# Where two groups of indirect gathers and the edge-row selection stand in the last two segments of a segmented attention kernel

## The chip, the cores and the metric

The kernel runs on one NeuronCore of a Trainium2 chip. The time is the device time of one execution in microseconds (us). Five engines work side by side, each through its own instruction stream in order: PE (matrix products), ACT (activations and copies), DVE (elementwise work and reductions), POOL (here it mostly issues indirect DMAs) and SP (plain DMAs). They meet only through semaphores.

## The reference, cut to what matters

```python
q, k, v = feat @ Wq, feat @ Wk, feat @ Wv            # feat: 16384 x 256
starts = searchsorted(bids, arange(8))               # bids are not sorted
pos = arange(N) - starts[bids]
qp, kp, vp = (zeros((8, 3072, .)).at[bids, pos].set(x) for x in (q, k, v))
attn = softmax(where(mask, qp @ kp^T, -1e9))         # within each of 8 segments
r = (attn @ vp)[bids, pos]
t = r @ Wt
tn = (t - t.mean(0)) / sqrt(t.var(0) + 1e-5) * gamma + beta
return feat + relu(tn)
```

Since `bids` is not sorted, most tokens have a `pos` outside 0..3071. Such tokens read the first or last row of a segment (the "edge" rows). Two tokens can also fall on the same place; the one that loses reads the winner's row. So each attention row is read some number of times, and the mean and the variance over all tokens are sums over attention rows weighted by how often each is read.

## The kernel before, in words

The fast path (`fast_path`, from L902) gathers the rows that own a place, segment by segment, into `xs`: up to six tiles of 128 rows for each of NB = 8 segments (FT = 6). In this data segment 7, and segment 6 too, have at most 512 rows, so the matmuls of their tiles 4 and 5 are skipped by predicates. Segment e is worked through in steps u = 0..5 (`step`, L1675): `attend` (L1270) multiplies the exponentiated scores `pa`/`pb` with the values `vs` into PSUM and DVE takes the reciprocal of the row sums into `rdens`; `scale` (L1285) writes the normalised rows `tk` (even u on ACT, odd u on DVE; in segment 7 all on ACT) and, after u = 3 and u = 5, SP stores them to the DRAM table `t_rows`. Between the steps of segment e stands the preparation of segment e+1: transposes `xT`, projections `q` and `k`, `values` and `scores`. Everything is written out by hand in one order; `Program.op` (L588) turns overlaps of tiles into semaphore waits, and each engine runs its own part of the order strictly in sequence.

For the moments, `past` (L1685) takes finished tiles from a list `lag`: ACT squares a tile (`square`, L1299), DVE adds the tile and its square into `acc`, weighted by the read counts `reads_r` (`moments`, L1329).

POOL's order in the last two segments matters here. It issues, one after the other:

- the read counts: `gather_reads(7, u)` (L1197), six gathers of 128 counts from the table `reads_of`, one in each `attend(6, u)`, each tied to that step's reciprocal (`paced`, L1279);
- `ridl`, three gathers of row numbers for the losing tokens;
- `late[1]`, that is `h` (L1627): six elementwise products on POOL that build the selection matrices `sel` from `edge`; `edge` comes from `late[0]`, that is `f` (L1598), a small matmul and a few small DVE instructions. Both stand after `step(6, 3)` (L1813);
- `tl`, the rows read a second time: three gathers from `t_rows`, rows of segments 0 to 5 only (L1829), after `step(6, 5)`. Line 1861 gathers them again from the whole table after the last segment, for the output;
- `ecat`, the edge rows: one gather from `t_rows` (L1743) in segment 7 after `step(7, 0)`, tied to `eidx`, the last instruction of `f`.

Segment 7 runs in the order u = 0, 1, 4, 5, 2, 3. After `step(7, 0)` the three `tl` tiles are put at the head of `lag` (L1752), so ACT squares `tl` next and DVE adds it. At u = 4 `weigh` (L1635) adds the read counts of tiles 2 and 3 to the edge weights, in `rw`. At u = 2 PE forms the edge rows of segment 7 (`sel` times `tk`, L1775), DVE adds them to `ecat` (L1778) and ACT squares `ecat`. After the last segment PE adds everything into `sums` (L1867, L1868), DVE transposes it (`st_t`, L1875), and a chain of small instructions gives scale and shift. Then the output phase starts: 16 groups of 1024 tokens are loaded, added, and stored by SP (`load_group`, `store`), while POOL scatters the 39 tiles of owned rows and losers (`put`), the tiles of a segment only when the group stores below it have landed.

SP also loads token groups during the last two segments: groups 0 to 2 in segment 6, groups 3 to 5 after `step(7, 0)` (L1744), group 6 after `step(7, 5)` (L1755), groups 7 to 9 after the loop. In the same queue stand the stores of `tk` to `t_rows`.

PSUM: `nb()` (L1050) hands out two banks in turn. `f`, `values`, `project`, `g` and `g2` take theirs from it.

Of the kernel before, what the change touches and what calls it, by code (L numbers as in the profile page):

```python
# [21 lines left out]
NB = 8  # L22
# [7 lines left out]
FW = FT * P  # L30
LT = 3
# [870 lines left out]
def fast_path(nc, feat, bids, wq, wk, wv, wt, gamma, beta, out, bad):  # L902
# [10 lines left out]
    pg = Fast(nc)  # L913
# [57 lines left out]
    xl, tl = new("xl", [P, LT, D]), new("tl", [P, LT, D])  # L971
# [16 lines left out]
    eidx, ridl, idxo = new("eidx", [P, 1], I32), new("ridl", [P, LT], I32), new("idxo", [P, LT], I32)  # L988
# [208 lines left out]
    def gather_reads(e, t, after):  # L1197
        m = e * FT + t
        pg.gather(reads_r[:, m : m + 1], reads_of, idx[:, m : m + 1], N, after=[after])

    def over4(e, t):
        return None if t < 4 else (e, t - 3)

# [40 lines left out]
    def values(e, c):  # L1244
        b = nb()
        for i in range(2):
            t = 2 * c + i
            for h in range(DH):
                pg.mm(
                    b[:, i * D : (i + 1) * D], xT[:, h, t * P : (t + 1) * P], wvt[:, h, :],  # L1250
                    start=(h == 0), stop=(h == DH - 1), pred=over4(e, t),
                )
        pg.copy("ACT", vs[e % 2][:, 2 * c : 2 * c + 2, 0:D], b[:].rearrange("p (t d) -> p t d", t=2))

    def scores(e, c, tiles):
        qe, ke = q[e % 2], k[e % 2]
        dst, n = (pa, QA) if c == 0 else (pb, QB)
        for t in tiles:
            g = slice(32 * (t % 4), 32 * (t % 4) + 32)
            pg.mm(  # L1260
                ps_s[t % 4][:, 0:n], ke[g, t // 4, :], qe[g, c * QA : c * QA + n],
                pred=over4(e, max(t, 4 * c)),
            )
        for t in tiles:
            m = e * FT + t
            pg.act(dst[:, t, :], ps_s[t % 4][:, 0:n], AF.Exp, bias=mask[:, m : m + 1])
# [3 lines left out]
    def attend(e, u):  # L1270
        po = po_of[u] = nb() if e == NB - 1 and u in (2, 3) else ps_o[u % 2]
        src, w = (pa, u) if u < 4 else (pb, u - 4)
        for t in (0, 1, 2, 4, 5, 3):
            pg.mm(
                po[:, 0 : D + 1], src[:, t, w * P : (w + 1) * P], vs[e % 2][:, t, :],
                start=(t == 0), stop=(t == 3), pred=over4(e, max(t, u)),
            )
        m = e * FT + u
        paced = pg.recip(rdens[:, m : m + 1], po[:, D : D + 1])  # L1279
        if EARLY_B <= e + 1 < NB:  # L1280
            gather_reads(e + 1, u, paced)
        if u % 2 and e < NB - 1:
            pg.ts(tk[:, m, :], po[:, 0:D], rdens[:, m : m + 1], ALU.mult)

# [390 lines left out]
    def step(e, u, more=None):  # L1675
        attend(e, u)
        if more is not None:
            more()
        scale(e, u)
        if (e, u) != (NB - 1, 1):  # L1680
            lag.append((e, u))
# [36 lines left out]
    for e in range(NB):  # L1718
        last = e == NB - 1
        n = e + 1  # L1720
        if e == 1:
            one, two, three_ = edges()
            sides = [*side_count(0, below[:]), *side_count(1, above[:])]
            fills = fill_rows()
            work.extend([fills[0], *one, fills[1], two, *sides, fills[2], *three_, lambda: own_of(NB - 1)])
        if not last:
            size_of(n)
        pg.region_of((e,) if last else (e, n))
        if e == 0:
            xt_rest(0)  # L1730
            values(0, 1)
            project(0, 1)
            values(0, 2)
            scores(0, 0, range(4, 6))
            own_of(2)
            zero_fill(2)
        if last:
            for u in (0, 1, 4, 5, 2, 3):
                step(e, u)
                if u == 0:  # L1740
                    scores(e, 1, range(4))
                    late[2]()
                    pg.gather(ecat[:, 0, :], t_rows[0 : (NB - 1) * FW, :], eidx[:], (NB - 1) * FW)  # L1743
                    for g in range(FIRST, EARLY):  # L1744
                        load_group(g)
                if u == 1:
                    scores(e, 1, range(4, 6))
                    late[4]()
                if u == 4:
                    late[3]()  # L1750
                if u == 0:
                    lag[:0] = [(NB, t) for t in range(LT)]  # L1752
                if u == 5:
                    first = square(e, 1)
                    for g in range(EARLY, MID):  # L1755
                        load_group(g)
                if u == 1:
                    pg.act(row_sum[:], ones[:], AF.Identity, scale=reads_r[:, e * FT + 1 : e * FT + 2])
                if u == 3:
                    any_ = hot[0 : 2 * NB, 0:2, :, :].rearrange("p k u x -> p (k u x)")  # L1760
                    pg.mm(sums[:], none[0 : 2 * NB, :], any_, start=True, stop=False)
                    by_row(row_sum, first[0], first[2])
                if u == 3:
                    while lag or squared:
                        if lag and len(squared) < 2:
                            squared.append(square(*lag.pop(0)))
                        else:
                            moments()
                else:
                    past(e)  # L1770
                if u == 2:
                    b_e = ps_s[0]
                    for u_ in (0, 4, 5, 1):
                        pg.mm(
                            b_e[:, 0:D], sel[:, u_, :], tk[:, e * FT + u_, :], start=(u_ == 0), stop=(u_ == 1),  # L1775
                            pred=over4(e, u_),
                        )
                    pg.tt(ecat[:, 0, :], ecat[:, 0, :], b_e[:, 0:D], ALU.add)  # L1778
                    pg.act(ecat[:, 1, :], ecat[:, 0, :], AF.Square)
        else:  # L1780
            busy = e + 2 < NB
            step(e, 0, lambda: (xt_main(n, 0), xt_main(n, 1)))
            if e + 3 < NB:
                prefix(e + 2, e + 3)
                sizes(e + 2)
            if busy:
                list_ahead(e + 2)
            scores(e, 1, range(4))
            past(e)
            slot()  # L1790
            if e == NB - 2:
                load_group(0)
            step(e, 1)
            xt_rest(n)
            project(n, 0)
            if busy:
                list_part(e + 2, 0)
            scores(e, 1, range(4, 6))
            past(e)
            slot(1 if busy else 2)  # L1800
            step(e, 2, lambda: project(n, 1))
            if busy:
                list_part(e + 2, 1)
            past(e)
            slot(1 if busy else 2)
            if e == NB - 2:
                slot(99)
                load_group(1)
                load_group(2)
            if e + 3 < NB:  # L1810
                zero_fill(e + 3)
            step(e, 3)
            if e == NB - 2:  # L1813
                late[0]()
                late[1]()
            scores(n, 0, range(4))
            step(e, 4, lambda: values(n, 0))
            past(e)
            if e + 4 < NB:
                own_of(e + 3)  # L1820
            if not busy:
                slot(2)
            if e == 3:
                losers()[0]()
            slot()
            step(e, 5)
            if e == NB - 2:
                for t in range(LT):
                    pg.gather(tl[:, t, :], t_rows[0 : EARLY_B * FW, :], ridl[:, t : t + 1], EARLY_B * FW)  # L1829
            values(n, 1)  # L1830
            past(e)
            if e == 3:
                losers()[1]()
            if e == NB - 4:
                prefix(NB - 1, NB)
                sizes(NB - 1)
                pg.copy("DVE", armf[:], arm[:])
                pg.red(cnt_f[0:1, 0:1], armf[:])
                pg.ts(upto[:, NB + 1 : NB + 2], cnt_f[0:1, 0:1], 16.0, ALU.mult, 16.0 * (4 * NB + LT), ALU.add)
                todo, late = rows()  # L1840
                work.extend(todo)
            scores(n, 0, range(4, 6))
            values(n, 2)
            past(e)
            slot()
        if last:
            assert not lag and not squared
        pg.end_region()
        if e == NB - 2:
            slot(99)  # L1850
            pg.set("POOL", none[:], 0.0)
# [227 lines left out]
```

## Time and profile before

| | |
|---|---|
| runs | 327.79 us median of 5 (327.03 to 328.62) |
| profiled execution | 326.57 us, of which the span from first to last instruction is 322.0 us |
| busy share of the span | PE 77%, DVE 74%, PEld 51%, ACT 47%, POOL 42% |
| mean granted TensorE clock | 0.893 |
| POOL groups | reads_r gather 12 times, 1056 ns each; tl gather 6 times, 1031 ns; ecat gather once, 1015 ns; sel 6 times, 858 ns |
| segments 0 to 6 | up to about 211 us |
| segment 7 and the sums | about 211 to 234.5 us |
| scale and shift | 234.5 to 241.9 us |
| output phase | 241.9 us to the end |

All times in what follows are microseconds from the start of the span. In the timeline and in the chain of waits, the first number is when an instruction (or a run of equal ones) starts and the second how long it lasts; a bracket gives how long its engine stood idle before it and what ended that. In the table by windows, the columns are the busy time of PE, PEld, DVE, ACT and POOL in a window (with the number of instructions), the granted TensorE clock (1.00 is full speed), the mean busy share of the 16 DMA engines, and GB/s.

### The profile page before, as it was taken

What the parts mean: (1) busy time and instruction counts of PE and PEld (TensorE: products, weight loads), DVE (VectorE), ACT (ScalarE), POOL (GpSimd) and SP (SyncE); (2) the same over time, 40 slices, a digit from 0 to 9 for tenths busy, and PEclk for the clock granted to TensorE, in tenths of its full rate; (3) what the DMA queues carried; (4) which work ended last, traced back from release to release, by engine and by line L of the source; (5) the groups of instructions that cost most, each with busy time, mean ns of one, the idle gap of its engine ahead of it and who ended that gap; (6) DMA issues with size and microseconds to landing.
All of it is one profiled execution on the core that took longest, in us unless ns stands there. A gap on an engine that the chain in (4) does not pass through costs nothing.

```text
span 322.0 us, 4632 instructions
## 1 busy us (share of the span) xinstructions
PE 247.8 (77%) x1279; PEld 163.2 (51%) x1279; DVE 239.3 (74%) x773; ACT 150.8 (47%) x294; POOL 135.9 (42%) x143
## 2 busy tenths in 40 slices
PE   5599799998998999899989999790956955642500
PEld 2465566666676678667866776470612322210100
DVE  3845679988577686569577898952879999999920
ACT  3037868775674674376448639671701221110000
POOL 7343316070170052404402563684030247878773
PEclk9999899999999999999999999797785797775755
DMA  3111104133063015301210134497598899999894
GB/s 103 29 29 34 34 2 136 43 105 93 0 124 132 0 51 135 95 0 52 71 35 1 51 108 139 166 344 283 189 413 327 302 381 423 417 415 380 331 379 170
DMA packets 21533, 52.49 MB, mean 163 GB/s; under 512 B 5488, under 2 KB 14786, under 8 KB 17530
## 3 DMA queue, kind: packets, MB, share of 16 engines
q1 hardware_dynamic: 15674, 41.37, 34.3%
q0 software_dynamic: 5280, 10.18, 10.8%
q10 hardware_dynamic: 544, 0.52, 0.5%
q8 instruction: 15, 0.25, 0.3%
q14 instruction: 20, 0.16, 0.1%
HBM read 26.27 MB, written 28.74 MB: 171 GB/s over the span
## 4 chain that ended last, share of the span: by engine, by line
PE 49%; DVE 21%; ACT 9%; issue 8%; POOL 7%; DMA 2%; another core or an unknown queue 1%; POOLq 1%; DVEq 0%; SPq 0%
PE ps L803 47%; POOL out L894 4%; DVE f L822 4%; DVE tk L822 4%; ACT pa L813 3%; PE ps L808 2%; DMA tl<-t_rows,ridl 2%; ACT xT L813 2%; ACT vs L818 2%; DVE junk L829 1%; DVE k L819 1%; DVE tk L1933 1%; DVE tk L1935 1%; ACT xs L818 1%
## 5 line engine op out<-in xcount | busy, mean ns | idle before, releaser
L878 POOL DMA_INDIRECT xs<-in_r_feat,idx x48 | 50.9, 1061 | 99.3 <-DVE idx L842 51.1
L803 PE MATMUL ps<-vs,pa 128*128 128x257 f32 x312 | 78.3, 396 | 4.1 <-ACT vs L818 3.8
L803 PEld LDWEIGHTS ps<-vs,pa 128*128 128x128 f32 x312 | 58.4, 195 | 18.0 <-ACT vs L818 6.2
L894 POOL DMA_INDIRECT out<-tk,idx x32 | 36.6, 1145 | 27.9 <-DVE f L822 15.9
L803 PE MATMUL ps<-wvt,xT 128*128 128x256 f32 x156 | 38.2, 393 | 0.7 <-ACT vs L818 0.7
L818 ACT COPY f<-ps 128x1024 f32<-128x1024 f32 (+1 forms) x12 | 10.0, 835 | 58.1 <-PE ps L803 58.1
L803 PE MATMUL ps<-y,hot 32*128 32x256 bf16 x256 | 14.5, 357 | 28.0 <-DVE f L822 19.9
L803 PEld LDWEIGHTS ps<-wvt,xT 128*128 128x128 f32 x156 | 29.6, 195 | 11.6 <-ACT sq L813 2.3
L813 ACT ACTIVATE pa<-ps,mask 128x512 f32<-128x512 f32 x48 | 29.5, 687 | 11.1 <-PE ps L803 10.3
L803 PEld LDWEIGHTS ps<-y,hot 32*128 32x128 bf16 x256 | 6.6, 113 | 44.8 <-DVE f L822 28.1
L803 PE MATMUL ps<-f,ident 128*128 128x512 f32 x38 | 27.3, 842 | 2.2 <-DVE f L822 1.2
L822 DVE TENSOR_TENSOR f<-f,ps 128x1024 f32<-128x1024 f32 (+3 forms) x17 | 26.0, 1560 | 3.8 <-remote 2.9
L819 DVE COPY k<-ps 32x128 f32<-32x128 f32 x48 | 14.1, 294 | 14.5 <-PE ps L803 13.8
L813 ACT ACTIVATE xT<-ps,negx 128x512 f32<-128x512 f32 (+1 forms) x32 | 16.9, 582 | 16.9 <-PE ps L808 10.0
L818 ACT COPY vs<-ps 128x512 f32<-128x512 f32 x24 | 14.1, 589 | 22.2 <-PE ps L803 17.4
L813 ACT ACTIVATE q<-ps,cqk 96x512 f32<-96x512 f32 (+3 forms) x32 | 18.3, 573 | 9.8 <-PE ps L803 9.5
L878 POOL DMA_INDIRECT reads_r<-reads_of,idx x12 | 12.7, 1056 | 24.3 <-DVE ge L831 11.7
L855 DVE RECIPROCAL rdens<-ps 128x1 f32<-128x1 f32 x48 | 7.7, 161 | 20.3 <-PE ps L803 20.3
L842 DVE SCALAR_TENSOR_TENSOR acc<-tk,reads_r,acc 128x256 f32<-128x256 f32 x45 | 21.6, 480 | 1.5 <-issue 1.3
L842 DVE SCALAR_TENSOR_TENSOR acc<-sq,reads_r,acc 128x256 f32<-128x256 f32 x45 | 21.5, 478 | 0.0
L813 ACT ACTIVATE pb<-ps,mask 128x256 f32<-128x256 f32 x48 | 19.2, 476 | 4.6 <-PE ps L803 4.5
L803 PE MATMUL ps<-xT,w 128*128 128x512 f32 (+1 forms) x48 | 20.7, 556 | 0.0
(271 smaller groups left out, 425.1 us busy)
## 6 DMA issues: line engine op xcount, KB each, us to landing
f<-in_r_feat SPq DMA_DIRECT2D x16, 1024.0 KB, 8.1
out<-f SPq DMA_DIRECT2D x15, 1024.0 KB
t_rows<-tk SPq DMA_DIRECT2D x8, 512.0 KB, 4.4
t_rows<-tk SPq DMA_DIRECT2D x8, 256.0 KB, 2.2
eb<-edge_of SPq DMA_DIRECT2D x16, 64.0 KB
out<-f SPq DMA_DIRECT2D x2, 512.0 KB, 2.7
xs<-in_r_feat,idx POOLq DMA_INDIRECT x48, 3.4
out<-tk,idx POOLq DMA_INDIRECT x39
```

Of the source, the lines that this page charges most:

```text
L803: "PE", lambda e: e.matmul(out, lhsT, rhs, start=start, stop=stop, skip_group_check=True),
L808: return self.op("PE", lambda e: e.transpose(out, in_, ident), [in_, ident], [out], pred=pred)
L813: "ACT", lambda e: e.activation(out, in_, func, bias=bias, scale=scale), [in_, *more], [out]
L818: return self.op("ACT", lambda e: e.copy(out, in_), [in_], [out])
L819: return self.op(eng, lambda e: e.tensor_copy(out, in_), [in_], [out])
L822: return self.op(eng, lambda e: e.tensor_tensor(out, a, b, op), [a, b], [out])
L829: lambda e: e.tensor_scalar(out, a, s1, s2, op0, op1, accum_out=accum)
L842: else e.scalar_tensor_tensor(out, a, s, b, op0, op1),
L855: return self.op("DVE", lambda e: e.reciprocal(out, in_), [in_], [out])
L878: lambda e: e.indirect_dma_start(out=out, out_offset=None, in_=table, in_offset=bass.IndirectOffsetOnAxis(ap=ind, axis=0), bounds_check=n ...
L894: lambda e: e.indirect_dma_start(out=table, out_offset=bass.IndirectOffsetOnAxis(ap=ind, axis=0), in_=src, in_offset=None, bounds_check=n ...
L1933: v.tensor_tensor(y, y, scale, ALU.mult).then_inc(sem, 1)
```

## The change

Three things move; no instruction is added or taken away.

1. The `tl` gathers (L1829, after `step(6, 5)`) go into `attend`: tiles 0 and 1 at u = 3 of segment 6, tile 2 at u = 4, each tied to that step's reciprocal.
2. The read counts of segment 7 are no longer one per step: tile 0 at u = 1, tile 1 at u = 2, tiles 2 and 3 at u = 4, tiles 4 and 5 at u = 5, in each step behind that step's `tl` gathers. Segment 6's own counts, gathered during segment 5, stay.
3. `late[0]` and `late[1]` (`f` and `h`) go from behind `step(6, 3)` to behind `step(6, 4)`, so behind `scores(7, 0)` and `values(7, 0)`.

```diff
+    def gather_again(t, after):
+        pg.gather(tl[:, t, :], t_rows[0 : EARLY_B * FW, :], ridl[:, t : t + 1], EARLY_B * FW, after=[after])
...
         paced = pg.recip(rdens[:, m : m + 1], po[:, D : D + 1])
-        if EARLY_B <= e + 1 < NB:
+        if e == NB - 3:
             gather_reads(e + 1, u, paced)
+        if e == NB - 2:
+            for t in ((), (), (), (0, 1), (2,), ())[u]:
+                gather_again(t, paced)
+            for t in ((), (0,), (1,), (), (2, 3), (4, 5))[u]:
+                gather_reads(e + 1, t, paced)
...
             step(e, 3)
+            scores(n, 0, range(4))
+            step(e, 4, lambda: values(n, 0))
             if e == NB - 2:
                 late[0]()
                 late[1]()
-            scores(n, 0, range(4))
-            step(e, 4, lambda: values(n, 0))
             past(e)
...
             step(e, 5)
-            if e == NB - 2:
-                for t in range(LT):
-                    pg.gather(tl[:, t, :], t_rows[0 : EARLY_B * FW, :], ridl[:, t : t + 1], EARLY_B * FW)
             values(n, 1)
```

## The prediction, made before the changed kernel was run

> **What bounds it now.** I read the waits between 186 and 242 us first, since all that moves lies there:
>
> ```profile
> PE ps L803 <- ACT pb L813: 8.4, 1, 8.4
> ...
> ACT sq L813 <- DMA tl<-t_rows,ridl: 8.1, 2, 7.5
> DVE acc L842 <- DMA tl<-t_rows,ridl: 7.8, 1, 7.8
> ```
>
> Three engines stand for about 8 us on one thing: ACT cannot square `tl`, so it cannot reach the scaled rows and exponentials behind it, so PE stands before its edge products. Then the chain of waits, which says whether this sets the end:
>
> ```profile
> 218.18 6.17 DMA tl<-t_rows,ridl
> ...
> 224.37 0.42 ACT sq L813
> 224.79 0.36 ACT tk L813
> 225.15 0.37 ACT pb L813
> ...
> 225.56 8.90 PE ps L803 x25
> ...
> 234.49 0.73 DVE st_t L858
> ```
>
> It does. From `st_t` the chain goes on in DVE to 240.9 and, after the first outputs, without a pause in DVE from 241.88 to 292.4; then POOL's scatters, back to back since 264.8, end it. Their start waits for group stores that DVE feeds. So a shift of `st_t` should reach the end whole, and the question is how far `st_t` moves. Next, POOL's timeline:
>
> ```profile
> 205.30 1.25 POOL L878 DMA_INDIRECT reads_r<-reads_of,idx  x1 [1.35 <-DVE k L819]
> 207.16 1.00 POOL L878 DMA_INDIRECT reads_r<-reads_of,idx  x1 [0.61 <-DVE zrow L842]
> 208.26 5.63 POOL L831 TENSOR_SCALAR sel<-edge,rcol 128x128 f32<-128x128 f32 x6
> 214.16 1.09 POOL L878 DMA_INDIRECT reads_r<-reads_of,idx  x1 [0.27 <-issue]
> 215.55 1.00 POOL L878 DMA_INDIRECT reads_r<-reads_of,idx  x1 [0.30 <-issue]
> 216.86 1.01 POOL L878 DMA_INDIRECT tl<-t_rows,ridl  x1 [0.31 <-issue]
> ...
> 220.88 1.01 POOL L878 DMA_INDIRECT ecat<-t_rows,eidx  x1 [0.16 <-issue]
> ```
>
> POOL has no slack from 207 to 222; `tl` is late because nine instructions stand before it. Last, clock and DMA:
>
> ```profile
> 217.00:218.00 1.00, 0.18 (x1) 0.00 (x0) 0.00 (x0) 0.00 (x0) 0.87 (x1) 1.00 0.94 385
> 222.00:223.00 1.00, 0.00 (x0) 0.00 (x0) 0.00 (x0) 0.00 (x0) 0.00 (x0) 0.58 0.72 258
> 223.00:224.00 1.00, 0.00 (x0) 0.00 (x0) 0.57 (x2) 0.42 (x1) 0.00 (x0) 0.50 0.34 126
> 224.00:225.00 1.00, 0.00 (x0) 0.00 (x0) 0.97 (x3) 0.63 (x2) 0.00 (x0) 0.50 0.02 8
> 228.00:229.00 1.00, 1.00 (x4) 0.81 (x3) 1.00 (x3) 0.92 (x3) 0.00 (x0) 0.51 0.10 34
> 229.00:230.00 1.00, 1.00 (x5) 0.62 (x4) 0.03 (x1) 0.72 (x2) 0.00 (x0) 1.00 1.27 327
> ```
>
> The DMA engines are full until 222 and empty from 224: the stall ends when the group loads drain. PE's clock halves 5 us after its last matmul (217.2) and returns 3.4 us after it restarts (225.56).
>
> **Step 1, POOL's new order.** The same instructions, reordered. At 207.16 the gather tied to the reciprocal of u = 3 (206.23) started; `tl` 0 now starts there. Gathers start 1.3 apart: `tl` at 207.2, 208.5, 209.8; counts 2 and 3 at 211.1 and 212.4; `sel` (5.63) from 213.5 to 219.1; counts 4 and 5 at 219.4 and 220.8; `ecat`, behind a small memset, at 222.2. `ecat` is 1.3 later than before, because counts 2, once issued at 205.3 ahead of this stretch, now stand inside it.
>
> **Step 2, the stall on `tl`.** A gather in full DMA traffic: the first `tl` went out at 216.86 and freed ACT at 223.40, 6.5 us; the second 6.2; the later ones 5.8. In quiet traffic counts land in 2.4. Even at 6.5, `tl` lands at 213.7, 215.0 and 216.3, before ACT is free (215.86, when its exponentials end). The stall of 7.5 + 0.55 goes.
>
> **Step 3, what is late next.** Without the stall DVE would reach the `ecat` addition (before: 228.62) near 220.7. But counts 4, which stand in front of it in DVE's order, land between 219.4 + 2.4 and 219.4 + 6.5, and `ecat`, out at 222.2, between 224.6 and 228.7. Behind that addition are queued the last reciprocal, the last counted tiles and the edge-weighted tiles; ACT's square of `ecat`, its last scaled tile, and SP's store and loads 7 to 9 wait for it too. So a new wait opens on DVE, and its size is the matter.
>
> I place `ecat`'s landing by the DMA load. Before, SP sent the store of tiles 4 and 5 at 227.97 and group 6 at 228.56, into empty engines. Both hang on ACT's scaled tile 5. That comes forward: `weigh` needs counts 3 (212.4 + 6.5 = 218.9), then 1.2 of DVE work, the reciprocal and 0.47 on ACT give 220.6, group 6 at 221.2. So 1.3 MB at about 400 GB/s, 3.3 us, join traffic that ended at about 223.6, and it now ends at 226.9. Before, `ecat` was out at 220.88 and down by 225.0 (the engines are at 0.02 in that window), at most 1.4 behind the end of the load; I take half, 0.7: `ecat` lands at L = 227.6, 5.4 after issue, inside the bounds 2.4 and 6.5.
>
> The Trainium skill, "DMA: Bandwidth & Descriptors", section "Anatomy of one DMA", gives an indirect DMA about 2.0 us plus bytes over 436 GB/s, and the section on queues lets each engine take turns between queues, so a gather should hardly notice the loads; an estimate by it lets `ecat` land near 224.5, with a gain of about 4 us. The 6.5 and 6.2 us of `tl` in this trace say otherwise, and I go by them.
>
> **Step 4, from `ecat` to `st_t`.** Addition 0.41, ACT's square 0.40, the scaled last tile 0.47: PE restarts at L + 1.35. Its work to `st_t` at full clock is half of the four records from 231.32 to 232.28 (0.5), the `ecat` product (1.05) and the `acc` product (1.15): 2.7. At half clock it doubles (the same four records took 2.08 at 225.56). DVE's own part (8 additions at 0.4) is done by L + 3.1, so at full clock `st_t` is at L + 4.25; at half throughout L + 6.6. PE is idle from about 221.6 to 229: the clock is at half when it restarts. If it returns after 3.4 us as before, 1.7 of the work is done by then and 1.0 is left: L + 5.75 = 233.35.
>
> The skill's page "TensorE: Matmul & The Clock Gate", Part 1, has free-running windows of about 3.4 us, so the return could come anywhere in a window; no row here fixes the phase. As an estimate by it, the end of this step would vary by about 1 us either way, and it speaks against any change that only moves PE's hole.
>
> **Step 5, `f` and `h` later.** PE's wait of 2.03 on `both` before 204.39 goes, and scores and values of segment 7 run at once. But `values(7, 1)` now shares its PSUM bank with `values(7, 0)`, with `f`'s bank between them, and must wait for ACT's copy. ACT frees at 205.5 (its scaled tile 2 hangs on DVE, unchanged), exponentials 2.4, copy 0.6: 208.45. PE ends it at 210.3 at full clock, 211.8 at half, against 211.16. From -0.9 to +0.7, hidden by the wait on `ecat`; uncovered it would come whole. I count 0.
>
> **Sum.** `st_t` from 234.49 to 233.35: 1.1 us gained of 8. The profiled execution (span 322.0, 4.6 around it, 326.57) would be 325.5. The median is 1.2 above that execution; less 1.1 it is **326.7**.
>
> **Rivals.**
>
> *Gathers land fast.* For it: 2.4 us for counts, and `ecat` itself, at most 4.1 before. Against: that was with loads draining, and group 6 now comes. With L between 224.6 and 226.3, middle 225.4: `st_t` at 231.2, gain 3.3, time 324.5. Best end 224.6: 4.1, time 323.7.
>
> *The hole only moves, and PE is cold through it* (slower). `ecat` takes the 6.5 us of the first `tl`, L = 228.7, and the clock stays at half to the end of the sums: 235.3, a loss of 0.8, time 328.6. It decides from L = 227.9 on (234.49 - 6.6), 5.7 after issue. For it: gathers of 5.8 and more whenever the loads were full. Against: the loads do end at 226.9.
>
> *The stall on `tl` stays*, because its gathers wait for something else (`ridl`, the table's stores): the transfer's start would have to slip by 2 us. `ridl` is issued by 201.3, the stores of segment 5 by 191.8. Time about 327.8; `ecat` would not move.
>
> **Chances.** Forecast (L 226.4 to 227.9) 0.50, its own range 0 to 2.3 gained (325.5 to 327.8); fast gathers 0.23; slower 0.19; no effect 0.08. The measurement tells 0.3%, 0.98 us, from no change. The forecast's half above that line (0.25) and the fast gathers (0.23) give faster 0.48; its other half and no effect, 0.33, are same; the slower case crosses the line only with a little more, but step 5 can add that, so I leave it 0.19. Bounds: 323.7 to 328.6, widened by half the spread of the runs upwards to 329.2 and by 0.1 downwards.
>
> **What would show it.** No wait of ACT on `tl`; in its place DVE waiting for `reads_r` and `ecat` around 221 to 228; `ecat` out at 222.2; group 6 near 221; PE idle near 222 to 229 at clock 0.5; `st_t` near 233.4. Wrong if the DVE wait ends by 225, if group 6 goes out after `ecat` has landed, or if the end does not follow `st_t`.

## The result and the profile after

| | before | changed |
|---|---|---|
| median of the runs | 327.62 us (58 runs) | 327.47 us (32 runs) |
| lowest to highest | 322.79 to 329.16 | 321.63 to 329.33 |
| profiled execution, its span | 326.57, 322.0 | 326.44, 321.7 |
| the same two kernels once more | 328.04 (11 runs) | 328.00 (6 runs), ratio 1.0009, 95% interval 0.9985 to 1.0034 |

The medians differ by 0.15 us, inside the 0.98 us that a measurement can tell from no change: the change does nothing measurable to a usual run. A comparison of the runs near each kernel's lowest in the first set gives a ratio of 0.99 (0.9868 to 0.9933), but it rests on a few runs some 5 us below the rest (5 of 32 changed, 1 of 58 before), which were never profiled, so I go by the medians and leave open why they are short and whether the change makes them more frequent.

The profiled execution of the changed kernel is 1.8 us late before the change begins: its reciprocal of u = 3 of segment 6 starts at 207.99, before's at 206.23. That gap is 1.44 already at the first reciprocal of all (37.35 against 35.91) and 1.65 at the fourth (53.34 against 51.69), in code that is the same in both. So I compare positions **behind that reciprocal**, called R, and the **stretch** from R to `st_t`: 28.26 us before, 26.97 after. The stretch leaves out such a gap, and it may not be chance: the first reciprocal lies at 35.9 to 36.5 in the four profiled kernels that leave `tl` where it was, and at 36.5 to 37.5 in the seven with the gathers moved as in the change. What makes it was not found, so a time can differ by up to about 1.6 us for a reason that the stretch doesn't show.

First the waits between 186 and 242 us of the changed kernel (line waited for: us in total, times, longest):

```profile
ACT sq L813 <- DVE acc L842: 2.8, 1, 2.8
PE ps L803 <- ACT vs L818: 2.7, 1, 2.7
DVE acc L842 <- DMA reads_r<-reads_of,idx: 2.6, 1, 2.6
...
DVE ecat L822 <- DMA ecat<-t_rows,eidx: 2.5, 1, 2.5
...
DVE rw L822 <- DMA reads_r<-reads_of,idx: 1.5, 1, 1.5
```

The wait on `tl` that held ACT and DVE for 8 us is gone, as meant. DVE now waits three times for other gathers: counts 3 (`rw`), counts 4 (`acc`) and `ecat`, 6.6 us in sum. POOL's timeline shows the new order:

```profile
209.02 1.00 POOL L878 DMA_INDIRECT tl<-t_rows,ridl  x1 [0.70 <-DVE zrow L842]
...
214.40 1.00 POOL L878 DMA_INDIRECT reads_r<-reads_of,idx  x1 [0.30 <-issue]
215.50 6.49 POOL L831 TENSOR_SCALAR sel<-edge,rcol 128x128 f32<-128x128 f32 x6
222.26 1.23 POOL L878 DMA_INDIRECT reads_r<-reads_of,idx  x1 [0.27 <-issue]
...
225.19 1.02 POOL L878 DMA_INDIRECT ecat<-t_rows,eidx  x1 [0.17 <-issue]
```

`sel` takes 6.49 us where it took 5.63, and `ecat` is out 17.2 us behind R (before: 14.7). The chain of waits now runs through it:

```profile
225.19 4.24 DMA ecat<-t_rows,eidx
229.44 0.43 DVE ecat L822
...
230.74 4.20 PE ps L803 x6
234.96 0.73 DVE st_t L858
```

The table by windows (columns as before the change) shows PE's clock and the DMA load around it:

```profile
224.00:225.00 1.00, 0.00 (x0) 0.00 (x0) 0.00 (x0) 0.18 (x1) 1.00 (x2) 1.00 0.88 280
225.00:226.00 1.00, 0.83 (x2) 0.42 (x3) 0.00 (x0) 0.00 (x0) 0.83 (x2) 0.55 1.04 275
...
228.00:229.00 1.00, 0.61 (x2) 0.00 (x0) 0.00 (x0) 0.00 (x0) 0.00 (x0) 0.74 0.35 133
229.00:230.00 1.00, 0.00 (x0) 0.00 (x0) 0.56 (x3) 0.10 (x1) 0.00 (x0) 1.00 0.00 0
...
231.00:232.00 1.00, 1.00 (x4) 0.32 (x3) 1.00 (x4) 0.98 (x2) 0.00 (x0) 0.96 0.36 123
232.00:233.00 1.00, 1.00 (x3) 0.16 (x1) 0.84 (x6) 0.49 (x1) 0.00 (x0) 0.50 1.03 332
```

The DMA engines run on until about 228.5, because group 6's load now goes out at 223.71, in front of `ecat`; `ecat` is added when they are empty. In this one execution the stretch is 1.3 us shorter, close to the forecast of 1.1. It isn't the usual case. The second run of the same kernel (327.97 us) has this chain:

```profile
221.99 6.74 DMA reads_r<-reads_of,idx
228.75 0.03 DVE acc L842
...
230.82 5.24 PE ps L803 x6
236.09 0.73 DVE st_t L858
```

Here the six `sel` took 7.11 us, group 6's load went out at 221.47, half a microsecond ahead of counts 4, and counts 4 needed 6.74 us to land. DVE's wait for them is 7.5 us: the whole hole of before, under another name. The stretch is 28.98.

### The profile page after: what moved, and what is told of

It reads as the page before. It is cut to its first block, busy times and chain, and to the rows that moved or that the text cites. A ratio compares the mean times of both kernels' runs of the same rounds, so it can differ in the third digit from the quotient of the medians.

```text
span 321.7 us, 4634 instructions
## 1 busy us (share of the span) xinstructions
PE 252.4 (78%) x1279; PEld 164.7 (51%) x1279; DVE 238.9 (74%) x773; ACT 151.0 (47%) x294; POOL 136.4 (42%) x143
## 4 chain that ended last, share of the span: by engine, by line
PE 43%; DVE 24%; ACT 11%; issue 10%; POOL 7%; DMA 1%; POOLq 1%; another core or an unknown queue 1%; DVEq 0%
PE ps L803 41%; DVE tk L822 6%; DVE f L822 5%; ACT pa L813 4%; POOL out L894 4%; PE ps L808 2%; ACT xT L813 2%; ACT vs L818 2%; DVE junk L829 1%; DMA ecat<-t_rows,eidx 1%; POOL sel L831 1%; DVE k L819 1%; DVE tk L1938 1%; DVE tk L1940 1%; POOLq L1072 1%
## 5 line engine op out<-in xcount | busy, mean ns | idle before, releaser
L803 PEld LDWEIGHTS ps<-vs,pa 128*128 128x128 f32 x312 | 58.0, 194 | 17.7 <-ACT vs L818 6.1
L894 POOL DMA_INDIRECT out<-tk,idx x32 | 34.9, 1089 | 29.4 <-DVE tk L842 20.2
L803 PE MATMUL ps<-y,hot 32*128 32x256 bf16 x256 | 14.6, 359 | 27.3 <-DVE f L822 23.3
L803 PEld LDWEIGHTS ps<-wvt,xT 128*128 128x128 f32 x156 | 28.9, 190 | 13.6 <-ACT vs L818 3.9
L803 PE MATMUL ps<-f,ident 128*128 128x512 f32 x38 | 28.5, 878 | 1.2 <-DVE f L822 1.2
L819 DVE COPY k<-ps 32x128 f32<-32x128 f32 x48 | 14.1, 294 | 15.7 <-PE ps L803 12.9
L813 ACT ACTIVATE xT<-ps,negx 128x512 f32<-128x512 f32 (+1 forms) x32 | 17.0, 582 | 17.2 <-PE ps L808 9.8
L842 DVE SCALAR_TENSOR_TENSOR acc<-tk,reads_r,acc 128x256 f32<-128x256 f32 x45 | 21.5, 477 | 4.1 <-DMA reads_r<-reads_of,idx 2.6
L855 DVE RECIPROCAL rdens<-ps 128x1 f32<-128x1 f32 x48 | 7.7, 160 | 19.6 <-PE ps L803 17.1
L803 PE MATMUL ps<-xT,w 128*128 128x512 f32 (+1 forms) x48 | 22.1, 586 | 0.0
L878 POOL DMA_INDIRECT reads_r<-reads_of,idx x12 | 13.3, 1110 | 19.8 <-DVE ge L831 11.7
L842 DVE SCALAR_TENSOR_TENSOR acc<-sq,reads_r,acc 128x256 f32<-128x256 f32 x45 | 21.5, 478 | 0.0
```

What stands on the lines that cost most here:

```text
L803: "PE", lambda e: e.matmul(out, lhsT, rhs, start=start, stop=stop, skip_group_check=True),
L813: "ACT", lambda e: e.activation(out, in_, func, bias=bias, scale=scale), [in_, *more], [out]
L819: return self.op(eng, lambda e: e.tensor_copy(out, in_), [in_], [out])
L842: else e.scalar_tensor_tensor(out, a, s, b, op0, op1),
L855: return self.op("DVE", lambda e: e.reciprocal(out, in_), [in_], [out])
L878: lambda e: e.indirect_dma_start(out=out, out_offset=None, in_=table, in_offset=bass.IndirectOffsetOnAxis(ap=ind, axis=0), bounds_check=n ...
```

## The experiments

My theory after the result was: the gathers moved ahead do free the 8 us, but the next gathers in POOL's order (counts 4 and 5, `ecat`) land late, and the later `sel` together with the earlier load of group 6 makes them so late that nothing is left. The main rival put the loss on PE: the later `f` makes `values(7, 1)` share a PSUM bank with `values(7, 0)`, PE stands for 2.7 us and its clock halves.

All twelve ran in three sets, each against the kernel before on the same chip. From each profiled execution, positions behind R, and the stretch, in us:

| kernel | median us (before in its set) | counts 4 out | ecat out | group 6 out | ecat added | stretch |
|---|---|---|---|---|---|---|
| before (profile shown first) | | 7.9 | 14.7 | 22.3 | 22.4 | 28.3 |
| changed (profile shown above) | | 14.3 | 17.2 | 15.7 | 21.5 | 27.0 |
| after_again | 328.00 (328.04) | 14.9 | 17.7 | 14.4 | 22.4 | 29.0 |
| gathers_only | 325.26 (328.04) | 13.4 | 16.1 | 19.6 | 20.0 | 26.6 |
| late_only | 328.05 (328.04) | 2.2 | 14.6 | 22.5 | 22.6 | 28.3 |
| group6_later | 325.39 (328.04) | 13.7 | 16.5 | behind the loop | 19.4 | 26.0 |
| h_later | 327.52 (328.06) | 13.7 | 16.6 | 15.5 | 22.1 | 28.6 |
| f_other_bank | 328.13 (328.06) | 12.8 | 15.8 | 15.3 | 22.7 | 29.3 |
| gathers_group6 | 325.44 (328.06) | 13.1 | 15.8 | behind the loop | 19.8 | 26.3 |
| counts_ahead | 322.34 (328.06) | -7.7 | 11.9 | 14.0 | 17.7 | 24.2 |
| counts_ahead_g6 | 321.80 (327.20) | -7.4 | 11.9 | behind the loop | 17.8 | 23.3 |
| counts_late_g6 | 321.71 (327.20) | -7.5 | 10.9 | behind the loop | 17.5 | 22.6 |
| counts_only | 324.63 (327.20) | -7.4 | 11.5 | 20.1 | 20.2 | 26.0 |
| before_g6 | 326.96 (327.20) | 7.7 | 14.5 | behind the loop | 22.6 | 28.9 |

A profile is one execution. Those of h_later (329.15 us) and f_other_bank (329.31 us) are the longest of their kernels' runs, that of the changed kernel (326.44 us) lies 1 us below its median.

Read the column "ecat added" against the medians: all kernels of 327 to 328 us have 21.5 to 22.7, those near 325 have 19.4 to 20.2, those near 322 have 17.5 to 17.8.

**after_again**: the changed kernel unedited.

> The changed kernel itself once more, for a second profile and more times. Measure: the stretch from the reciprocal of step 3 of segment 6 to st_t, which leaves out what differs upstream from execution to execution: before 206.23 to 234.49, 28.3 us; after 207.99 to 234.96, 27.0 us. Theory (the wait on ecat takes the place of the wait on tl, and the rest is gained): stretch 27.0 within 1 us, and the time about 1.2 us below the kernel before. Rival (the stretch gets shorter, but the end does not follow st_t): same stretch, time within 0.3 us of the kernel before.

It gave 328.00 us against 328.04, and the chain shown above. Both theories had the stretch near 27.0 us, and it is 28.98; the time is that of the rival.

**gathers_only**: the gathers moved as in the change, `f` and `h` where they were.

```diff
             step(e, 3)
+            if e == NB - 2:
+                late[0]()
+                late[1]()
             scores(n, 0, range(4))
             step(e, 4, lambda: values(n, 0))
-            if e == NB - 2:
-                late[0]()
-                late[1]()
```

> The gathers moved as in the change, f and h left behind step 3. POOL's order is then tl 0, tl 1, sel, tl 2, counts 2 to 5, ecat. Theory (what ends the stretch is when counts and ecat land, and f and h are hidden): no wait of ACT on tl 0 and 1, DVE waits for counts 3 until about 17 us after the reciprocal of step 3, group 6 goes out late, into emptier engines, stretch 26.5 to 27.5 us. Rival (the later place of f and h is what makes the gain, by the wait on both that it removes): stretch near 28.3 us.

325.26 us, ratio 0.9915 (0.989 to 0.994): the gathers alone gain 2.8 us. Its waits say why:

```profile
DVE rw L822 <- DMA reads_r<-reads_of,idx: 6.7, 1, 6.7
...
ACT sq L813 <- DMA tl<-t_rows,ridl: 5.3, 3, 4.5
```

`sel` stands in the middle of the moved gathers here, counts 2 and 3 go out behind it, and DVE waits 6.7 us for counts 3. That wait holds back the last reciprocals, ACT's scaled tile 5, and with it group 6's load (19.6 behind R, later than `ecat` at 16.1). Counts 4 and `ecat` then don't have group 6's load in front of them: after this wait DVE has no other for a gather of counts or edge rows.

**late_only**: `f` and `h` moved, the gathers as before (the edits of `attend` and of L1829 undone).

> Only f and h moved behind step 4; all gathers as in the kernel before. Theory: tl still goes out after nine other POOL instructions, about 10.6 us after the reciprocal of step 3, ACT waits for it about 8 us, stretch 28.3 us within 0.7, time within 0.7 us of before. Rival (f and h make the gain): stretch near 27.0 us, time 1.2 us below before.

328.05 us, ratio 0.9996 (0.9964 to 1.0028). ACT still waits 6.8 us for `tl`; under that wait the later `f` and `h` cost nothing.

**group6_later**: the whole change, with group 6's load behind the loop.

```diff
                 if u == 5:
                     first = square(e, 1)
-                    for g in range(EARLY, MID):
-                        load_group(g)
...
-    for g in range(MID, NF):
+    for g in range(EARLY, NF):
         load_group(g)
```

> The changed kernel with the load of token group 6 taken from behind step 5 of segment 7 to the loads of groups 7 to 9, behind the loop, so that it no longer runs beside the last gathers. Theory (the earlier load of group 6 holds ecat up): ecat lands 2 to 3 us after its issue instead of 4.2, and the wait on it ends about 2 us earlier, stretch about 25 us. Rival (ecat is late by POOL's queue alone, and loads do not matter): landing unchanged at 4.2, stretch 27.0 us. If the end follows st_t, the time falls by as much as the stretch.

325.39 us, ratio 0.993 (0.9903 to 0.9957). DVE's lines in its timeline:

```profile
226.50 0.48 DVE L842 SCALAR_TENSOR_TENSOR acc<-tk,reads_r,acc 128x256 f32<-128x256 f32 x1 [3.74 <-DMA reads_r<-reads_of,idx]
...
227.38 0.42 DVE L822 TENSOR_TENSOR ecat<-ecat,ps 128x256 f32<-128x256 f32 x1
```

`ecat`, out at 224.50, is there at 227.38 at the latest, 2.9 us after issue; with group 6 in front it took 4.2 (the changed kernel), 4.8 at most (after_again), 5.5 and 6.9 (the next two). The DMA engines are down to 0.16 in the window from 225; in the changed kernel they run on until 228. The stretch is 26.0 us and not the 25 expected: counts 4, out at 221.65, still took 4.9 us.

**h_later**: the change, but `f` back behind `step(6, 3)`; only `h` stays late.

```diff
             step(e, 3)
+            if e == NB - 2:
+                late[0]()
             scores(n, 0, range(4))
             step(e, 4, lambda: values(n, 0))
             if e == NB - 2:
-                late[0]()
                 late[1]()
```

> The changed kernel with f's pair of matmul and copy put back behind step 3 of segment 6 and only h (whose sel is POOL's long compare) left behind step 4. TensorE's order up to step 4 is that of the kernel with the gathers alone, POOL's order is that of the whole change. Theory A (the later f costs its time through the shared PSUM bank: TensorE's hole of 2 to 2.7 us ahead of values(7,1) and the half clock after it): about 325.3 us as with the gathers alone, the reciprocal of step 0 of segment 7 about 5.2 us behind that of step 3 of segment 6, stretch to st_t about 26.5 us. Theory B (the later sel costs it through POOL's queue: counts 4 and 5 and ecat pushed back until group 6's load is in front of them): about 327.7, counts 4 about 14 us behind the reciprocal, ecat about 17, stretch 27 to 29 us.

327.52 us (12 runs) against 328.06 (27 runs), no interval given. PE has no hole at the shared bank and its clock stays full to 225, yet the time of gathers_only doesn't come back, and the stretch is 28.6. This is theory B's number.

**f_other_bank**: the whole change, `f`'s small product in a bank of the output pair.

```diff
-            ps = nb()
+            ps = ps_o[1]
```

> The whole change, with f's small matmul written to a PSUM bank of the output pair instead of the next bank of the ring, so that values(7,1) no longer takes the bank of values(7,0). Theory A (the shared bank): TensorE's wait of 2.7 us on ACT's copy goes, reciprocal of step 0 of segment 7 at 5.2 to 6 us instead of 7.56, time about 325.5. Theory B (POOL's order): the wait goes and the end doesn't move, about 327.5, with counts 4 still out at about 14 us and ecat at 17.

328.13 us, ratio 0.9997 (0.9974 to 1.0021). PE's timeline of the changed kernel first:

```profile
210.10 2.50 PE L803 MATMUL ps<-wvt,xT 128*128 128x256 f32 x8 [2.72 <-ACT vs L818]
```

and of f_other_bank:

```profile
208.48 0.39 PE L803 MATMUL ps<-both,ones 128*128 128x16 f32 x2 [1.67 <-DVE tk L831]
208.75 1.99 PE L803 MATMUL ps<-wvt,xT 128*128 128x256 f32 x8
```

The wait of 2.72 is gone, `values(7, 1)` starts 1.0 us behind R instead of 2.1, and the next reciprocal 5.5 instead of 7.6. Then DVE stands for the same gathers:

```profile
225.87 0.48 DVE L842 SCALAR_TENSOR_TENSOR acc<-tk,reads_r,acc 128x256 f32<-128x256 f32 x1 [3.10 <-DMA reads_r<-reads_of,idx]
...
230.44 0.42 DVE L822 TENSOR_TENSOR ecat<-ecat,ps 128x256 f32<-128x256 f32 x1 [3.69 <-DMA ecat<-t_rows,eidx]
```

The rival falls: PE's hole is hidden.

**gathers_group6**: gathers_only with group 6's load behind the loop (both edits above).

> The gathers moved, f and h as before the change, and group 6's load behind the loop. If group 6's load in front of the counts is what costs the time wherever it happens, little is left to win here, since in the kernel with the gathers alone that load went out at 19.6 us, behind ecat: 325 us, within 0.3 us of the gathers alone. If the two gains add up (2.7 of the gathers, 2.6 of group 6), about 322.7.

325.44 us, ratio 0.9931 (0.9907 to 0.9955): the two gains don't add, since they are two ways to the same thing: group 6's load isn't in front of `ecat`.

**counts_ahead**: gathers_only with the six counts of segment 7 issued at the start of segment 6, where POOL is idle, and all three `tl` at u = 3.

```diff
     def attend(e, u):
+        if (e, u) == (NB - 2, 0):
+            for t in range(FT):
+                gather_reads(e + 1, t, None)
...
-            for t in ((), (), (), (0, 1), (2,), ())[u]:
+            for t in ((), (), (), (0, 1, 2), (), ())[u]:
                 gather_again(t, paced)
-            for t in ((), (0,), (1,), (), (2, 3), (4, 5))[u]:
-                gather_reads(e + 1, t, paced)
```

> f and h as before the change, the six counts of segment 7 all issued at the start of segment 6 where POOL is idle, the three tl behind step 3. Nothing is then queued between sel and ecat. If the landing of the counts is what fills the hole that the change opened, ecat is out about 11 to 12 us behind the reciprocal instead of 16 to 17.5, the wait for counts goes, stretch 22 to 24 us, time about 322 to 324 us. If the path from the attention steps to ecat is itself no shorter (DVE and ACT bound), the stretch stays at 26 and the time at 325.

322.34 us (321.41 to 323.44), ratio 0.9833 (0.9801 to 0.9865): 5.7 us faster than before. `ecat` is out at 11.9, no wait for counts is left, and the stretch is 24.2, just past the 22 to 24 expected: `ecat` still took 5.9 us.

**counts_ahead_g6**: the same with group 6 behind the loop.

> The kernel with the counts ahead (322.34 us), with group 6's load behind the loop as well. There ecat was out at 11.85 us behind the reciprocal of step 3 and added at 17.71: 5.9 us, with group 6's load out 2.2 us behind it. With group 6 behind the loop the gather of edge sums took 2.9 us in the kernel group6_later. If group 6's load costs the landing whatever else waits, ecat is added some 3 us earlier and the time falls to about 319.5 to 320. If the store of tile 5's rows or the queue itself makes those 5.9 us, the landing stays and the time with it, 322.

321.80 us (320.41 to 323.34) against 327.20. That is 5.4 below its before, counts_ahead 5.7 below its own: no gain, and the expected 319.5 to 320 is a miss. `ecat` went out at 219.03. The windows and DVE's line of this kernel:

```profile
221.00:222.00 1.00, 1.00 (x5) 0.71 (x5) 0.73 (x2) 0.91 (x3) 0.00 (x0) 1.00 1.01 426
222.00:223.00 1.00, 0.89 (x5) 0.44 (x3) 0.00 (x0) 0.20 (x1) 0.00 (x0) 1.00 0.99 417
223.00:224.00 1.00, 0.00 (x0) 0.00 (x0) 0.00 (x0) 0.00 (x0) 0.00 (x0) 1.00 0.91 333
224.00:225.00 1.00, 0.00 (x0) 0.00 (x0) 0.00 (x1) 0.00 (x0) 0.00 (x0) 1.00 0.31 111
```

```profile
225.00 0.42 DVE L822 TENSOR_TENSOR ecat<-ecat,ps 128x256 f32<-128x256 f32 x1 [3.27 <-DMA ecat<-t_rows,eidx]
```

PE, DVE, ACT and POOL all stand from 222.9 to 225.0, and `ecat` comes in the window in which the DMA engines empty. No group 6 is there; what fills them are groups 3 to 5, issued from 212.73 on (and, 1.6 us behind the gather, the store of tiles 4 and 5). So the loads that were in flight before the gather was issued seem to hold it as well. That is read from the trace; a kernel without those loads was not run.

In counts_ahead, for comparison, group 6 went out 2.2 us behind `ecat`. The gather took the same 5.9 us, and `ecat` was added while that load still filled the DMA engines:

```profile
224.00:225.00 1.00, 0.00 (x0) 0.00 (x0) 0.70 (x3) 0.24 (x1) 0.00 (x0) 1.00 1.05 433
```

```profile
224.30 0.42 DVE L822 TENSOR_TENSOR ecat<-ecat,ps 128x256 f32<-128x256 f32 x1 [3.17 <-DMA ecat<-t_rows,eidx]
```

So a load behind the gather didn't hold it here; with group 6 in front, as in the changed kernel, the addition came only with the engines empty.

**counts_late_g6**: counts_ahead_g6 with `f` and `h` behind `step(6, 4)`, as in the change.

> The same with f and h behind step 4, as in the change: the price of step 5 of the prediction where neither tl, nor the counts, nor group 6 can cover it. By the prediction it is -0.9 to +0.7 us against the kernel counts_ahead_g6; by the later place of sel in POOL's queue ecat goes out later, by up to 1.5 to 2 us if sel starts that much later, and the time follows.

321.71 us (320.87 to 323.32) against 321.80: no cost. PE's hole of 2.7 us is there again, `sel` takes 5.18, `ecat` is out 1.0 earlier and added 0.4 earlier. With the counts out of POOL's way, moving `f` and `h` is free.

**counts_only**: the kernel before with nothing but the six counts ahead; `tl` stays behind `step(6, 5)`.

> The kernel before, with only the six counts of segment 7 issued ahead; tl where it was, behind step 5, f and h where they were. If the wait for tl and the wait for the counts each hide the other, this gains nothing: ACT's wait of about 7 us on tl stays, 327.5 to 328.3 us. If the counts alone were the limit, about 322.

324.63 us (324.09 to 325.86) against 327.20. A miss: I expected the `tl` stall to stay whole. Its waits:

```profile
ACT sq L813 <- DMA tl<-t_rows,ridl: 5.8, 2, 5.3
DVE acc L842 <- DMA tl<-t_rows,ridl: 5.6, 1, 5.6
```

With no counts 4 and 5 ahead of it and no step to wait for, the first `tl` goes out 7.2 us behind R instead of 10.6, and the stall shrinks from 7.5 to 5.3. A part of the stall on `tl` was the counts' doing.

**before_g6**: the control, the kernel before with group 6's load behind the loop.

> Control: the kernel before with nothing but group 6's load behind the loop. If that load costs time only where it goes out ahead of counts 4 and ecat, it gains nothing here, where it went out at 22.33 us, as ecat was being added: 327.8 +- 0.4. If loads behind the loop are a gain by themselves, 325.5.

326.96 us (325.91 to 328.47) against 327.20: nothing to tell from no change. Loads behind the loop are no gain by themselves.

## Why the prediction was right and where it was wrong

The time lay 0.8 us from the forecast, inside the range, but the gain of 1.1 us did not come in a usual run: 0.15 and 0.04 by the medians. The range, about 323.6 to 329.2 us, takes in all of the rivals' times too, and the prediction gave a faster kernel 0.48 and an unchanged one 0.33, so that the time came out close says little about the mechanism. By steps:

- **What bounds it** held. `tl` held three engines, its wait ended when it was moved, and `st_t` carries the end: over the profiled executions of this study the span ends 86.6 to 88.2 us behind `st_t`, while the stretch went from 22.6 to 29.3.
- **Step 1** had the order right and `sel` too short: 6.49 and 7.11 us in the two executions, not 5.63. `ecat` went out 17.2 and 17.7 behind R; the prediction's 222.2 is 16.0.
- **Step 2** held: no wait on `tl`. (By its own figures the third `tl`, at 216.3, lands after ACT is free at 215.86 and not before; ACT squares it only at 219.5, and nothing came of it.)
- **Step 3** named the right mechanism, counts 4 and `ecat` behind an earlier group 6, and is the step that failed, in its size. It put `ecat`'s landing at 227.6, 21.4 behind R, only 0.3 us from the point at which its own slower rival decides (227.9, 21.7 behind R), and took `ecat` as the gather that lands last. In the profiled changed kernel the addition came at 21.45, on the forecast, but by luck: `ecat` went out 1.2 us later than forecast and took 4.2 us instead of 5.4. In after_again counts 4 alone landed at 21.6, behind two additions the `ecat` addition came at 22.4, on the rival's side. With the same POOL order h_later (22.1) and f_other_bank (22.7) are there too. Of the four profiles with the late `sel` and group 6 in place, three took the rival's path (two of them the longest executions of their kernels). With `sel` 0.9 to 1.5 us longer than assumed in the two of the changed kernel, and gathers under load at 3.8 to 6.9 us, a margin of 0.3 us settled nothing. group6_later, which takes only that load away, brings 2.6 us.
- **Step 4** gave lengths that were measured, but not by the course that it assumed. From the start of the `ecat` addition to `st_t` the changed kernel took 5.5 us and after_again 6.55, where the prediction chose 5.75 and gave 6.6 for half clock throughout (its own terms, 1.35 and twice 2.7, add up to 6.75). It had PE idle from 221.6 to 229, at half clock at the restart and at full clock 3.4 us later. In the profiled changed kernel PE worked from 225.2 to 228.6, on products that had waited for POOL's memset, and its clock was back at full within the window from 228 and stayed so until the end of that from 231: PE restarts at full clock at 230.7 and falls to half behind it. That 5.5 lies near 5.75 is luck. In after_again the clock is down to 0.84 in the window from 230 and to 0.50 from 231 on, as PE restarts. The rival's 235.3 is 29.1 behind R; after_again has 28.98. The Trainium skill, "TensorE: Matmul & The Clock Gate", Part 1, has the clock judged in free-running windows of about 3.4 us. The means of the windows from 225, 228 and 231 (0.55, 0.74, 0.96) put its changes at 225.1, 228.5 and 231.9 in the changed kernel, 3.4 us apart, which agrees, and so does a spread of 1 us in this step from one execution to the next.
- **Step 5** was right: hidden, counted 0. PE's wait at the shared bank is 2.7 us, and taking it away (f_other_bank) or putting `f` back (h_later) brings nothing. The cover is the wait for the gathers; counts_late_g6 shows that it still covers with the counts gone. What the later `h` costs is not on PE. It lies in POOL's order, through steps 1 and 3: `sel` behind counts 2 and 3 lets those land early, DVE runs on, and group 6 comes in front of `ecat`, in after_again of counts 4 too.
- **The rivals.** Fast gathers did not happen as described: with the load in front, none landed in 2.4 us. The skill's fixed 2.0 us plus bytes ("DMA: Bandwidth & Descriptors", "Anatomy of one DMA") is not far from the 2.9 at most of group6_later, where the load had gone, and far from the 6.7 of after_again. The slower rival's mechanism is what most profiled executions show; as a loss of 0.8 us against one profiled execution of before it hardly shows, because that execution is a short one (326.57 us against a median of 327.62; the control before_g6 has a stretch of 28.9).

Open: what makes a gather wait for the loads issued before it was not taken apart, and neither was what sets the length of `sel`.

## What to carry to other kernels

When a late gather is moved forward on an in-order queue, ask what was queued with it and issue the gathers that wait for nothing (here the counts, a table that was ready long before) in an idle stretch of that queue; this gave 5.7 us where the move itself gave none. Follow the freed wait to the loads that it releases: a plain load that comes forward by 7 us in front of a small gather can take the whole gain. If the forecast stands 0.3 us from the point at which its own rival decides, and the rows behind it spread by 1 us, it is an even bet and should be priced as one.

## What the runs showed of the hardware that I had not expected

- A small indirect gather has no fixed price: `ecat` took at most 2.9 us with the DMA engines emptying (group6_later), and counts 4 and `ecat` 3.8 to 6.9 with 1 MB loads around them. In these profiles a load issued in front of a gather held it, one issued behind it did not. In h_later, counts 4 went out 1.8 us ahead of group 6's load and were used 4.8 us later, with the DMA engines at 1.01 in that window; `ecat`, out 1.1 us behind the load, was there only with the engines empty, after 5.5 us. In f_other_bank it was 5.3 us for counts 4 and 6.9 for `ecat`. Counts_ahead, above, says the same.
- POOL's six `sel` took 5.08 to 7.11 us for the same work in the profiles of this study (5.63 before, 6.49 and 7.11 in the changed kernel). I did not find what sets it.
- The length of a hole on PE doesn't settle whether its clock falls. A hole of 2.7 us (207.4 to 210.1) was followed by half clock from 211.4 to 214.9 in the changed kernel; the same hole at the same place in group6_later was not, and the clock stayed at full. One of 2.0 us was followed by half clock in the kernel before (202.4 to 204.4, half from 205.1 to 208.5), and not in gathers_only (204.0 to 206.1).
